# Selective scan on one core: the causal convolution as four shifted projections, D u as a diagonal product, and one output projection for each direction

## The chip, the core and the metric

The kernel runs on one core of a Trainium2 chip. The metric is the device time of one execution in microseconds, the median of several runs. All figures here come from the profile of one execution and from the times of the runs. TensorE is written PE, VectorE DVE, ScalarE ACT, GpSimd POOL and SyncE SP, as in the profile. L1392 is line 1392 of the kernel before.

## The reference

The program is a network of twelve blocks in a row: attention over a context with ternary weights, a bidirectional selective scan ("mamba"), grouped and expert feed-forward layers, three kinds of attention, a recurrent mixer. Only the scan block and the lines that prepare it change. The activations are 4 sequences of 128 tokens with 128 channels (512 tokens in all). The scan block adds to x the sum of two passes over the normalized x, one over the tokens in order and one over the tokens reversed (the reversed pass is turned back). One pass is, with 256 inner channels, 16 states and 4 taps:

```python
xi, z = jnp.split(x @ in_w.T, 2, axis=-1)
xc = conv_general_dilated(xc, conv_w, padding=[(3, 0)], feature_group_count=di)   # causal, 4 taps per channel
xc = silu(xc + conv_b)
x_dbl = xc @ xp_w.T                     # 8 columns dt, 16 of B, 16 of C
delta = softplus(dt @ dtp_w.T + dtp_b)
A = -jnp.exp(A_log)
h = h * exp(d_t * A) + (d_t * u_t) * b_t          # for each token, 256 x 16 states
y = einsum('bdn,bn->bd', h, c_t)
y = (y + xc * Dp) * silu(z)
return y @ out_w.T
```

## The kernel before

The program is written with Tile: the code gives instructions in program order, a scheduler lays them out in one fixed queue for each engine when the kernel is built, and semaphores are put in where a tile is handed over. The queue of an engine is not quite the order of the code (two dbu of neighbouring iterations stand next to one another at 210.23 us, ahead of the scans of the first), but on the chip each engine takes its queue as it stands. Tiles come from pools with a fixed number of buffers; a new tile of a pool waits until the one that it takes the place of has been read.

Everything in `mamba` is laid out with channels on partitions and the 512 tokens on the free axis. The 256 inner channels of a direction are two halves of 128. The stage runs from about 174 to 357 us of the span.

- **The pools.** All PSUM results except y and dA (xd_ps, xi_ps, z_ps, xdbl_ps, dt_ps, b_ps, c_ps, out_ps) come from one ring of three tiles, `ps`. y has its own tile of two halves, dA has three tiles. SBUF tiles of setup have two buffers, those of the loop (cs, dbu, h, hc) three.
- **setup(d)**, a generator, makes u, zs, x3, delta and du of a direction. Its first step transposes the normalized x with matmuls into xd_ps (L1304; with a flip for direction 1) and copies it to xT. For each half follows xi_ps (L1314, one matmul in fp32, two instructions in the profile), a copy by ScalarE into a tile with three zeros ahead of each sequence (pad, L1317), and the convolution on VectorE: one multiply by a scalar (L1321) and three multiply-adds (L1323). Silu on ScalarE gives u (L1325). Then z_ps and its silu (L1331, L1333), the projection xdbl_ps of u (L1337), copies of dt and x3 on VectorE (L1341 on; x3 is kept as three bf16 parts), dt_ps (L1355), the softplus (L1236 to L1255), and du = delta times u (L1363).
- **The loop.** For each direction and each of the 16 states n: b_ps and c_ps spread row n of B and of C over the partitions (L1368, PE), ACT copies c_ps to cs (L1381), DVE makes dbu = du times b_ps (L1383), ACT makes dA = exp(delta A) for each half (L1389), DVE scans each half (h, L1392), POOL multiplies h by cs (hc, L1395), and PE adds hc to y by a product with the identity (L1397, two fp32 matmuls). setup(1) is advanced by one step in each iteration from n = 2 of direction 0 on (`got = next(ahead, got)`), so all of its instructions stand among the loop's on every queue.
- **The end of a direction.** For each half, yd = u D + y on DVE (L1405) and yT = yd times zs (L1407).
- **The end of the stage.** After direction 1, 16 matmuls of 128x128 (two profile records each) project both directions into out_ps (L1413), and DVE adds it to x (L1416). The next stage (`grouped_ffn`) first reads x for its layer norm and loads ew from HBM on ACT's queue (L1430); SP's queue has the transfers r_qk and r_vo (L473), ctx (L1233), and w_r (L318).

`busy` (L389) issues matmuls with no use for the result, seven of them ahead of the first transpose. `load` fetches a weight tile once; the one of the scan block holds in_w, xp_w and out_w of both directions in one tile. In `bit_attention`, the stage before, several units of attention are processed in a loop over i, and after it a short chain (absmax, quantize to qf and qa, matmuls with ternary weights) ends the stage. `zero_after` makes a zero that depends on another value, so that what uses it waits.

Of the kernel before, what the change touches and what calls it, by code (L numbers as in the profile page):

```python
# [18 lines left out]
P = 128  # L19
B = 4  # L20
# [126 lines left out]
def _layout(i):  # L147
# [58 lines left out]
    def xp(m):  # L206
# [4 lines left out]
            i["L0_attn_in_w" + d].T, xp(i["L0_attn_xp_w" + d]), kchunks(i["L0_attn_out_w" + d].T))],  # L211
        axis=1,
    )
    a["dtp"] = np.concatenate([m.T for m in both("dtp_w")], axis=1)
    a["l0f"] = np.concatenate([i["L0_ffn_w1"], kchunks(i["L0_ffn_w2"])], axis=1)

# [55 lines left out]
class Net:  # L272
# [39 lines left out]
    def load(self, name):  # L312

        if name not in self._w:
            shape = list(self.A[name].shape)
            lo = XP - shape[0] if name == "dtp" else 0
            t = self.wp.tile([lo + shape[0]] + shape[1:], F32, tag="w", name="w_" + name)
            self.nc.sync.dma_start(t[lo:], self.A[name])  # L318
            self._w[name] = t
        return self._w[name]  # L320

    def copy(self, out, in_):
# [612 lines left out]
    def bit_attention(self, nxt):  # L935
# [4 lines left out]
        with ExitStack() as es:  # L940
# [211 lines left out]
            for i, u in enumerate(units):  # L1152
                u.top()
                if i + 1 < len(units):
                    units[i + 1].scores(0)
                u.spread()
                u.weights(0)
                u.weights(1)
                if i:
                    units[i - 1].values()  # L1160
                if i + 1 < len(units):
                    units[i + 1].scores(1)
                if i + 2 < len(units):
                    units[i + 2].queries()
                if i == 2:
                    ternary(ps, 5, 7)
                if i in (3, 4):

                    half = NS // 2
                    lo = (i - 3) * half  # L1170
                    mw = wk.tile([P, 1024], I32, tag="qtmp", name="mask")
                    nc.sync.dma_start(
                        mw[DC:AUG], self.A["mask"][:, lo // 4 : (lo + half) // 4].partition_broadcast(3)[:, 0])
                    aug = self.k("augs")[DC:AUG]
                    nc.gpsimd.tensor_scalar(
                        self.ctxT[DC:AUG, lo : lo + half], mw.bitcast(U8)[DC:AUG], aug[:, 0:1], aug[:, 1:2],
                        ALU.mult, ALU.add)
# [12 lines left out]
            self.quantize(wk, avg, qa, inv)  # L1190
            qab = one.tile([P, B, T], BF16, name="qab")
            nc.vector.tensor_copy(qab, bc_in(qa, T))
            hT = big.tile([P, BIG], F32, tag="big", name="hT")[:, 0 : 4 * N].rearrange("p (m n) -> p m n", m=4)
            osc = out_scale("f1", s)
            for m in range(4):
# [40 lines left out]
    def softplus(self, pool, out, vs, biases, first):  # L1236
# [4 lines left out]
        e = pool.tile([P, len(vs), N], F32, tag="sp_e", name="sp_e")  # L1241
        for i, (v, bias) in enumerate(zip(vs, biases)):
            nc.scalar.activation(e[:, i], v, AF.Abs, bias=bias)
            nc.vector.tensor_scalar(out[:, i], v, bias, 0.0, ALU.add, ALU.max)
        nc.scalar.activation(e, e, AF.Exp, scale=-1.0)
        s = pool.tile([P, len(vs), N], F32, tag="sp_s", name="sp_s")
        nc.vector.tensor_scalar_add(s, e, 1.0)
# [6 lines left out]
        nc.scalar.activation(s, s, AF.Ln)  # L1254
        nc.vector.tensor_add(out, out, s)  # L1255

    def mamba(self, nxt):

# [5 lines left out]
        with ExitStack() as es:  # L1266
# [17 lines left out]
            for j in range(3):  # L1284
                t = das.tile([P, B, T], F32, name=f"dA{j}")
                nc.vector.memset(t[:, :, 0:1], 0.0)
                dAs.append(t)
            turn = 0
            xn = one.tile([P, B, C], F32, name="xn")
            self.layernorm(self.x, xn)  # L1290
            yT = one.tile([P, 2, 2, N], F32, name="yT")
# [4 lines left out]
            def setup(d):  # L1296
# [6 lines left out]
                for b in range(B):  # L1303
                    nc.tensor.matmul(  # L1304
                        tr[:, b * T : b * T + T], xn[:, b], self.k("flip") if d else self.ident,
                        start=True, stop=True)
                xT = tp.tile([P, N], F32, tag="xT", name="xT")
                self.copy(xT, tr)
                yield
                u = wk.tile([P, 2, N], F32, tag="u", name="u")  # L1310
                for half in range(2):
                    i = d * 2 + half
                    mm = mm_tile("xi_ps")
                    nc.tensor.matmul(mm, w[:, at + half * P : at + half * P + P], xT, start=True, stop=True)  # L1314
                    pad = wk.tile([P, B, T + 3], F32, tag="pad", name="pad")
                    nc.gpsimd.memset(pad[:, :, 0:3], 0.0)
                    nc.scalar.copy(pad[:, :, 3:], mm.rearrange("p (b t) -> p b t", b=B))  # L1317
                    yield
                    cw = self.col("conv_w")[:, i * 4 : i * 4 + 4]
                    acc = wk.tile([P, B, T], F32, tag="conv", name="conv")  # L1320
                    nc.vector.tensor_scalar_mul(acc, pad[:, :, 0:T], cw[:, 0:1])  # L1321
                    for k in range(1, 4):
                        nc.vector.scalar_tensor_tensor(  # L1323
                            acc, pad[:, :, k : k + T], cw[:, k : k + 1], acc, ALU.mult, ALU.add)
                    nc.scalar.activation(  # L1325
                        u[:, half], self.flat(acc), AF.Silu, bias=self.col("conv_b")[:, i : i + 1])
                    yield
                zs = wk.tile([P, 2, N], F32, tag="z", name="z")
                for half in range(2):
                    mm = mm_tile("z_ps")  # L1330
                    nc.tensor.matmul(  # L1331
                        mm, w[:, at + 256 + half * P : at + 256 + half * P + P], xT, start=True, stop=True)
                    nc.scalar.activation(zs[:, half], mm, AF.Silu)  # L1333
                yield
                mm = mm_tile("xdbl_ps")
# [2 lines left out]
                        mm[:XP], w[:, at + 512 + half * XP : at + 512 + (half + 1) * XP], u[:, half],  # L1338
                        start=half == 0, stop=half == 1)
                dt = tp.tile([XP, N], F32, tag="dt", name="dt")  # L1340
                nc.vector.tensor_copy(dt[96:XP], mm[96:XP])  # L1341
                x3 = wk.tile([96, N], BF16, tag="x3", name="x3")
                r = tp.tile([96, N], F32, tag="x3r", name="x3r")
                nc.vector.tensor_copy(x3, mm[:96])
                nc.vector.tensor_sub(r[32:64], mm[32:64], x3[32:64])
                nc.vector.tensor_sub(r[64:96], mm[64:96], x3[64:96])
                nc.vector.tensor_copy(x3[32:64], r[32:64])
# [18 lines left out]
            def spread(x3, n, name):  # L1366
                mm = mm_tile(name)
                nc.tensor.matmul(mm, sel[:, n : n + 1].to_broadcast([96, P]), x3, start=True, stop=True)  # L1368
                return mm

            for got in setup(0):
                pass
            for d in range(2):
# [3 lines left out]
                for n in range(16):  # L1377
# [17 lines left out]
                    nc.gpsimd.tensor_mul(hc, h, bc_mid(cs, 2))  # L1395
                    for half in range(2):
                        nc.tensor.matmul(y[:, half], self.ident, hc[:, half], start=n == 0, stop=n == 15)  # L1397
                    if n > 1:
                        got = next(ahead, got)
                for got in ahead:  # L1400
                    pass
                for half in range(2):
                    i = d * 2 + half
                    yd = tp.tile([P, N], F32, tag="yd", name="yd")
                    nc.vector.scalar_tensor_tensor(  # L1405
                        yd, u[:, half], self.col("D")[:, i : i + 1], y[:, half], ALU.mult, ALU.add)
                    nc.vector.tensor_mul(yT[:, d, half], yd, zs[:, half])  # L1407
            out = mm_tile("out_ps").rearrange("p (b t) -> p b t", b=B)
            for b in range(B):
                for i in range(4):  # L1410
                    d, half = divmod(i, 2)
                    at = d * MW + 512 + 2 * XP + half * P
                    nc.tensor.matmul(  # L1413
                        out[:, b], yT[:, d, half, b * T : b * T + T], w[:, at : at + P],
                        start=i == 0, stop=i == 3)
            nc.vector.tensor_add(self.x, self.x, out)  # L1416

    def grouped_ffn(self, nxt):

# [831 lines left out]
```

## Time and profile before

| | us |
|---|---|
| median of the runs | 1392.51 (1391.57 to 1392.85, three runs) |
| the profiled execution's own time | 1393.84 |
| its span | 1391.7 |
| scan stage in the span | 174 to 357 |
| first dbu to the end of the last scan | 203.48 to 345.52 |
| last scan to the end of the residual add | 345.52 to 356.95 |

The granted TensorE clock is 0.916 of full speed over the whole span. In the stage the two directions' 64 scans and 32 dbu are the largest items of DVE, hc of POOL, and y of PE; dA is the largest of ACT.

How to read the lines that follow: in a group, "out<-in" are the program's tile names with shapes, then count, total busy time and mean time of one in nanoseconds, and after the second bar the time that its engine stood idle just before and the instruction that released it. In a timeline, the first number is the start, the second the duration, and the bracket at the end holds the idle time before. "x2" or more means neighbouring instructions joined.

### The profile page before, as it was taken

The numbers are of one execution on the slowest core, as the hardware profiler recorded it, in microseconds if no ns is written. First come the engines' busy times: TensorE is split into PE (matmuls) and PEld (weight loads), VectorE is DVE, ScalarE is ACT, GpSimd is POOL, SyncE is SP. The second block draws the span as 40 slices with busy tenths as digits, with TensorE's granted clock in tenths as the row PEclk, the third lists the DMA queues.
The fourth block names the chain that finished last, engine by engine and source line by source line (L and its number), as shares of the span: only waits on it lengthen the run. The fifth ranks groups of instructions, "written<-read, shape, count | busy, mean of one in ns | idle before, by whom it ended". The sixth has DMA issues, their size and how long they took to land.

```text
span 1391.7 us, 15803 instructions
## 1 busy us (share of the span) xinstructions
PE 1149.7 (83%) x6204; PEld 604.2 (43%) x6204; DVE 914.2 (66%) x1596; ACT 627.0 (45%) x848; POOL 205.9 (15%) x187
## 2 busy tenths in 40 slices
PE   2477557677899999999998944899987889999978
PEld 0156422222644444444433424476342454666644
DVE  7988779899348666776676698512564776554535
ACT  3743256444346555665553410233542761545432
POOL 0026205357000001000000430000122200000000
PEclk9988768789999999999999976799998988999978
DMA  6000000000700000000000100330000000000010
GB/s 188 0 1 2 1 1 0 30 0 0 211 0 1 0 0 0 1 0 0 1 1 0 61 0 1 104 75 23 0 0 7 7 7 0 2 1 2 3 57 8
DMA packets 9485, 27.82 MB, mean 20 GB/s; under 512 B 1191, under 2 KB 7120, under 8 KB 8350
## 3 DMA queue, kind: packets, MB, share of 16 engines
q1 hardware_dynamic: 8286, 24.88, 6.2%
q10 hardware_dynamic: 1120, 1.88, 0.4%
q8 instruction: 51, 0.84, 0.3%
q14 instruction: 28, 0.23, 0.1%
HBM read 26.49 MB, written 0.26 MB: 19 GB/s over the span
## 4 chain that ended last, share of the span: by engine, by line
PE 61%; DVE 19%; ACT 5%; issue 5%; POOL 3%; DVEq 0%; ACTq 0%; POOLq 0%
PE sc L590 12%; PE av L614 12%; PE s_ps L780 5%; DVE h L1392 3%; PE t_ps L804 2%; PE k_ps L706 2%; PE h_ps L1831 2%; PE y_ps L1843 2%; PE av L817 2%; PE mm L1478 2%; PE y_ps L1397 1%; DVE dbu L1383 1%; PE q_ps L542 1%; POOL hc L1395 1%; POOL mbs L606 1%
## 5 line engine op out<-in xcount | busy, mean ns | idle before, releaser
L614 PE MATMUL av<-s,ctx 128*97 128x512 f32 x448 | 210.4, 601 | 11.6 <-ACT s L612 11.0
L590 PE MATMUL sc<-q_aug,ctxT 99*128 99x512 f32 x448 | 206.2, 592 | 0.0
L611 DVE TENSOR_TENSOR s<-s,mbs 128x1024 f32<-128x1024 f32 x112 | 133.0, 1220 | 39.0 <-POOL mbs L606 39.0
L592 ACT COPY s<-sc 128x1024 f32<-128x1024 f32 x112 | 112.3, 1003 | 80.7 <-PE sc L590 80.7
L612 ACT ACTIVATE s<-s 128x1024 f32<-128x1024 f32 x112 | 116.2, 1057 | 63.1 <-DVE s L611 62.8
L600 DVE TENSOR_TENSOR m<-m,s 128x1024 f32<-128x1024 f32 x72 | 88.2, 1225 | 75.0 <-ACT s L592 75.0
L590 PEld LDWEIGHTS sc<-q_aug,ctxT 99*128 99x128 f32 x448 | 84.6, 189 | 110.2 <-issue 91.3
L614 PEld LDWEIGHTS av<-s,ctx 128*97 128x97 f32 x448 | 72.5, 166 | 124.1 <-issue 103.6
L784 DVE TENSOR_REDUCE na_m<-s_ps 128x1 f32<-128x512 f32 x128 | 82.2, 686 | 61.9 <-PE s_ps L780 61.7
L606 POOL PARTITION_ALL_REDUCE mbs<-m x20 | 35.7, 1785 | 488.4 <-DVE m L602 488.4
L810 ACT ACTIVATE p<-t_ps 128x1024 f32<-128x1024 f32 x64 | 62.0, 1021 | 85.4 <-PE t_ps L804 85.4
L1397 PE MATMUL y_ps<-hc,consts 128*128 128x512 f32 x128 | 75.6, 724 | 29.2 <-POOL hc L1395 27.7
L1395 POOL TENSOR_TENSOR hc<-h,cs 128x1024 f32<-128x1024 f32 x32 | 75.7, 2378 | 84.1 <-DVE h L1392 84.1
L780 PE MATMUL s_ps<-kT,q 32*128 32x512 f32 x256 | 81.9, 682 | 1.0 <-DVE na_m L784 0.9
L1392 DVE TENSOR_TENSOR_SCAN h<-dA,dbu 128x512 f32<-128x512 f32 x64 | 74.2, 1205 | 4.1 <-ACT dA L1389 3.9
L1397 PEld LDWEIGHTS y_ps<-hc,consts 128*128 128x128 f32 x128 | 26.1, 223 | 82.0 <-POOL hc L1395 56.4
L804 PE MATMUL t_ps<-q,kT 32*128 32x128 f32 x1024 | 57.0, 287 | 1.2 <-ACT p L810 1.2
L1389 ACT ACTIVATE dA<-delta,A 128x508 f32<-128x508 f32 x64 | 42.8, 687 | 29.5 <-DVE h L1392 29.3
L804 PEld LDWEIGHTS t_ps<-q,kT 32*128 32x128 f32 x1024 | 48.6, 189 | 11.2 <-issue 7.0
L393 PEld LDWEIGHTS <-consts 128*128 128x128 bf16 x160 | 17.6, 120 | 67.4 <-issue 51.3
L1847 DVE SCALAR_TENSOR_TENSOR x<-y_ps,cw,x 128x128 f32<-128x128 f32 x32 | 9.0, 345 | 50.3 <-PE y_ps L1843 44.4
L780 PEld LDWEIGHTS s_ps<-kT,q 32*128 32x128 f32 x256 | 28.1, 194 | 25.4 <-DVE na_m L784 14.8
(599 smaller groups left out, 1949.5 us busy)
## 6 DMA issues: line engine op xcount, KB each, us to landing
w_moe<-in_moe SPq DMA_DIRECT2D x2, 2048.0 KB, 9.6
ctxT<-in_ctxT SPq DMA_DIRECT2D x3, 768.0 KB
w_l3f<-in_l3f SPq DMA_DIRECT2D x1, 1920.0 KB, 8.1
rows<-in_rows ACTq DMA_DIRECT2D x1, 1664.0 KB, 13.7
w_l0f<-in_l0f SPq DMA_DIRECT2D x1, 1024.0 KB
w_mamba<-in_mamba SPq DMA_DIRECT2D x1, 976.0 KB, 18.3
w_r<-in_r SPq DMA_DIRECT2D x1, 960.0 KB
consts<-in_consts SPq DMA_DIRECT2D x1, 832.0 KB, 16.6
```

The lines of the kernel that those rows point to most:

```text
L590: nc.tensor.matmul(sc[:, i], self.ctxT[:, at : at + P], u.q, start=True, stop=True)
L592: nc.scalar.copy(s, sc)
L600: nc.vector.tensor_max(u.m, u.m, u.s[j])
L611: nc.vector.tensor_sub(p, p, bc_mid(u.mb, 2))
L612: nc.scalar.activation(p, p, AF.Exp)
L614: nc.tensor.matmul(u.av[: DC + 1], self.ctx[:, u.b * NCH + chunks[2 * j + i]], p[:, i], start=j + i == 0, stop=j == n - 1 and i == 1)
L780: nc.tensor.matmul(t, qs[rows], kT[rows, s, j * 512 : j * 512 + 512], start=True, stop=True)
L784: nc.vector.tensor_reduce(part[:, at : at + 1], t, axis=AX, op=ALU.max, negate=True)
L804: nc.tensor.matmul(ts[g // 2][:, g % 2, j], kT[g * 32 : g * 32 + 32, s, at : at + P], qs[g * 32 : g * 32 + 32], start=True, stop=True)
L1392: nc.vector.tensor_tensor_scan(h[:, half], self.flat(dA), dbu[:, half], 0.0, ALU.mult, ALU.add)
L1395: nc.gpsimd.tensor_mul(hc, h, bc_mid(cs, 2))
L1397: nc.tensor.matmul(y[:, half], self.ident, hc[:, half], start=n == 0, stop=n == 15)
```

## The change

- **Weights.** A 1 MB array `taps` with the convolution weights for each of four (direction, half) pairs and four taps, laid along the free axis, is added to the inputs. `load` fetches it to all partitions with a second transfer into the tile of the scan block. The load is called in `bit_attention` at i == 3. Weights of the projection times tap k give a stationary matrix for each tap (`conv_weights`): for half 0 of direction 0 VectorE computes it at the end of `bit_attention`, for the two halves of direction 1 POOL does so at the start of `mamba`.
- **The convolution.** For three of the four (direction, half) pairs, four matmuls with the tap matrices and the shifted padded xT accumulate the convolution in one PSUM tile, and silu reads it there. Half 1 of direction 0 keeps the convolution on VectorE. xT is written straight into the padded tile: for direction 0 one half by VectorE and one by ScalarE, for direction 1 by ScalarE.
- **ScalarE for direction 1.** The copies of dt and of x3 and the relu of the softplus go to ScalarE.
- **D u.** A diagonal matrix of D (`dd`, one multiply on POOL) times u is accumulated into y by two matmuls at n == 3 of each direction; yT is then y times zs.
- **The output projection.** Direction 0 is projected and added to x at n == 4 of direction 1, direction 1 at the end of the stage.

```diff
+    a["taps"] = np.concatenate([w.reshape(2, P, 4).transpose(0, 2, 1).reshape(-1) for w in both("conv_w")])[None]
@@ load
+            more = 16 * P if name == "mamba" else 0
+            t = self.wp.tile([lo + shape[0], shape[1] + more], F32, tag="w", name="w_" + name)
+            self.nc.sync.dma_start(t[lo:, : shape[1]], self.A[name])
...
+                taps = t[:, shape[1] :]
+                self.nc.sync.dma_start(taps, self.A["taps"].partition_broadcast(P)[:, 0])
@@ bit_attention
+                if i == 3:
+                    self.load("mamba")
...
             nc.vector.tensor_copy(qab, bc_in(qa, T))
+            self.conv_weights(0, self.taps[:, 0], s)
@@ softplus
-            nc.vector.tensor_scalar(out[:, i], v, bias, 0.0, ALU.add, ALU.max)
+            if first:
+                nc.vector.tensor_scalar(out[:, i], v, bias, 0.0, ALU.add, ALU.max)
+            else:
+                nc.scalar.activation(out[:, i], v, AF.Relu, bias=bias)
+    def conv_weights(self, i, out, x=None):
+        w, taps = self._w["mamba"], self.taps[:, i]
...
+        if x is None:
+            self.nc.gpsimd.tensor_mul(out, taps, w)
+        else:
+            self.nc.vector.scalar_tensor_tensor(out, taps, self.zero_after(x, "cv_z"), w, ALU.add, ALU.mult)
@@ mamba
+            cv = one.tile([P, 2, 4, P], F32, name="cvw")
+            for half in range(2):
+                self.conv_weights(2 + half, cv[:, half])
+            cvw = [self.taps[:, 0], None, cv[:, 0], cv[:, 1]]
+            for d in range(2):
+                pads.append(one.tile([P, B, T + 3], F32, name=f"pad{d}"))
+                nc.gpsimd.memset(pads[d][:, :, 0:3], 0.0)
+            dd = one.tile([P, 4, P], F32, name="dd")
+            nc.gpsimd.tensor_mul(dd, bc_mid(self.ident, 4), bc_in(self.col("D"), P))
...
-                xT = tp.tile([P, N], F32, tag="xT", name="xT")
-                self.copy(xT, tr)
+                xT = pad[:, :, 3:]
+                if d == 0:
+                    nc.vector.tensor_copy(xT[:, 0:2], tr[:, 0:2])
+                    nc.scalar.copy(xT[:, 2:4], tr[:, 2:4])
+                else:
+                    nc.scalar.copy(xT, tr)
                 yield
...
+                for half in (0, 1) if d else (1, 0):
...
+                    if i == 1:
...
+                    for k in range(4):
+                        nc.tensor.matmul(to, cvw[i][:, k], pad[:, :, k : k + T], start=k == 0, stop=k == 3)
+                    mms.append((half, mm))
+                    if d:
+                        silu(*mms.pop())
                     yield
...
-                nc.vector.tensor_copy(dt[96:XP], mm[96:XP])
+                (nc.scalar.copy if d else nc.vector.tensor_copy)(dt[96:XP], mm[96:XP])
-                nc.vector.tensor_copy(x3, mm[:96])
+                (nc.scalar.copy if d else nc.vector.tensor_copy)(x3, mm[:96])
...
+            def project(d):
+                out = mm_tile("out_ps").rearrange("p (b t) -> p b t", b=B)
+                for b in range(B):
+                    for half in range(2):
+                        at = d * MW + 512 + 2 * XP + half * P
+                        nc.tensor.matmul(
+                            out[:, b], yT[:, d, half, b * T : b * T + T], w[:, at : at + P],
+                            start=half == 0, stop=half == 1)
+                nc.vector.tensor_add(self.x, self.x, out)
...
                     for half in range(2):
                         nc.tensor.matmul(y[:, half], self.ident, hc[:, half], start=n == 0, stop=n == 15)
+                    if n == 3:
+                        for half in range(2):
+                            nc.tensor.matmul(y[:, half], dd[:, d * 2 + half], u[:, half], start=False, stop=False)
+                    if n == 4 and d:
+                        project(0)
                     if n > 1:
                         got = next(ahead, got)
...
-                    yd = tp.tile([P, N], F32, tag="yd", name="yd")
-                    nc.vector.scalar_tensor_tensor(
-                        yd, u[:, half], self.col("D")[:, i : i + 1], y[:, half], ALU.mult, ALU.add)
-                    nc.vector.tensor_mul(yT[:, d, half], yd, zs[:, half])
-            out = mm_tile("out_ps").rearrange("p (b t) -> p b t", b=B)
...
+                    nc.vector.tensor_mul(yT[:, d, half], y[:, half], zs[:, half])
+            project(1)
```

## Prediction

> **What bounds the kernel now.** I read the page's chain first: the span is mostly TensorE, and the stage that changes, from about 174 to 357 us, is one part of it. So I went to the costliest groups whose lines lie in that stage.
>
> ```profile
> PE 61%; DVE 19%; ACT 5%; issue 5%; POOL 3%; DVEq 0%; ACTq 0%; POOLq 0%
> ...
> L1397 PE MATMUL y_ps<-hc,consts 128*128 128x512 f32 x128 | 75.6, 724 | 29.2 <-POOL hc L1395 27.7
> L1395 POOL TENSOR_TENSOR hc<-h,cs 128x1024 f32<-128x1024 f32 x32 | 75.7, 2378 | 84.1 <-DVE h L1392 84.1
> L1392 DVE TENSOR_TENSOR_SCAN h<-dA,dbu 128x512 f32<-128x512 f32 x64 | 74.2, 1205 | 4.1 <-ACT dA L1389 3.9
> L1389 ACT ACTIVATE dA<-delta,A 128x508 f32<-128x508 f32 x64 | 42.8, 687 | 29.5 <-DVE h L1392 29.3
> ```
>
> The scans on VectorE waited 4.1 us in all; TensorE, GpSimd and ScalarE waited for them far longer. VectorE sets the pace of the scan loop. The table of stretches says how tight that is:
>
> ```profile
> 203.50:244.00 40.50, 28.93 (x61) 11.79 (x61) 38.43 (x35) 24.19 (x36) 19.53 (x8) 0.79 0.00 1
> 244.00:282.00 38.00, 24.67 (x43) 8.13 (x41) 30.85 (x31) 17.29 (x25) 12.65 (x6) 0.76 0.08 28
> 282.00:350.00 68.00, 49.10 (x112) 17.78 (x112) 63.29 (x58) 30.07 (x50) 43.54 (x19) 0.95 0.00 0
> ```
>
> The first number after the stretch is its length, then PE, PE loads, DVE, ACT, POOL busy, and the clock granted to TensorE. VectorE is busy 38.4 of 40.5 us in the first stretch, but TensorE already has 28.9 there at a mean clock of 0.79: room for about 11 us more, if its order allows it.
>
> In the undisturbed loop (first of each pair of dbu at 308.34, 315.06, 321.78) two iterations take 6.72 us, all VectorE: 32 iterations are 107.5 of the 142.0 us from the first dbu (203.48) to the end of the last scan (345.52). The other 34.5 are about 25 us of the second direction's setup and the first one's gating on VectorE, and 9.3 of its idle time.
>
> **What comes off VectorE.** In the groups of VectorE inside the loop:
>
> ```profile
> L1323 DVE SCALAR_TENSOR_TENSOR conv<-pad,cols,conv 128x512 f32<-128x512 f32 x6 | 6.3, 1050 | 0.0
> L1321 DVE TENSOR_SCALAR conv<-pad,cols 128x512 f32<-128x512 f32 x2 | 2.9, 1450 | 0.0
> L1244 DVE TENSOR_SCALAR delta<-dt_ps,cols 128x512 f32<-128x512 f32 x2 | 1.4, 734 | 0.0
> ```
>
> By the steps between starts, the eight convolution instructions cost 8.6 us (some wait for GpSimd before they work). dt and x3 move to ScalarE (0.73 + 0.61), so do the two relus (1.3): 11.2 us of VectorE saved in direction 0's loop. In direction 1 two yd (L1405) and their handoff go: 2.2. Were VectorE still the only limit, this and the tail would be the gain.
>
> **What TensorE gets, and in which order.** Direction 1's convolution becomes eight fp32 matmuls in place of two, the D u product two per direction. In TensorE's queue of the changed program, what stands ahead of the fourth iteration's b_ps (on which dbu, and so both scans wait) is: two shifted matmuls, y of n=2 and of n=3, two D u, two shifted matmuls, b_ps. Before, one xi_ps stood there, and the y's came after:
>
> ```profile
> 217.12 0.38 PE L1368 MATMUL b_ps<-x,sel 96*128 96x512 bf16 x1
> ...
> 217.54 1.22 DVE L1383 TENSOR_TENSOR dbu<-du,b_ps 128x1024 f32<-128x1024 f32 x1 [0.51 <-PE b_ps L1368]
> 217.56 1.88 PE L1397 MATMUL y_ps<-hc,consts 128*128 128x512 f32 x4
> ...
> 219.60 1.98 PE L1397 MATMUL y_ps<-hc,consts 128*128 128x512 f32 x4 [0.16 <-POOL hc L1395]
> ```
>
> A warm fp32 matmul of 512 columns is two records 0.43 apart, 0.86 us. I replayed the queues by hand with these durations:
> - n=4: y of n=3 starts at 219.60 as before; then six matmuls (y 2, D u 2, shifted 2) of 0.86 and a b_ps of 0.43: dbu at 225.4 instead of 217.54. VectorE has no other ready work, so it stands still about 8.4 us.
> - n=5: three shifted matmuls, then y of n=4, one shifted, b_ps. Its y needs the whole chain: dbu 1.2, two scans 2.3, hc 2.36, y 1.72, shifted 0.86, b_ps 0.43, so dbu of n=5 comes 9 us after that of n=4 where 3.36 is the work: a stall of 5.6. The ring of three PSUM tiles gives no slack: the xi tile holds a place.
> - n=7: y of n=5 and the first xdbl ahead of it: 3.2.
>
> That is 17 us of new waits. Against it stand the 11.2, and some of the old 9.3 us of stalls (before, 1.83 for xdbl_ps, and 2.67 and 1.56 around the table loads), which either shrink or lie beside the new ones. ScalarE gets two more table loads (1.28 each, silu and exp three times in place of two) and 2.7 us of copies and relus, less two pad copies of 0.59; it is busy 24 of 40 us, so only those on the dA path count, which my replay has. The replay puts dbu of n=14 at 279.9 to 281.0, with warm clock, and 280.9 is where it was.
>
> **A rule on the clock.** The replay's chain hc, y, b_ps leaves TensorE idle 2.3 us at a time. The trace, in the table of stretches and the timeline:
>
> ```profile
> 238.40:241.80 3.40, 1.45 (x4) 0.26 (x2) 2.44 (x3) 3.14 (x5) 1.99 (x1) 1.00 0.00 0
> 241.80:245.20 3.40, 2.98 (x4) 1.43 (x5) 2.34 (x2) 2.42 (x4) 0.75 (x2) 0.50 0.00 0
> ...
> 242.22 3.46 PE L1397 MATMUL y_ps<-hc,consts 128*128 128x512 f32 x4 [1.23 <-POOL hc L1395]
> ```
>
> A window with 1.45 us of matmuls, no gap in it longer than 1.23, was followed by one at half clock, where the y pair cost 3.46 in place of 1.98. The Trainium skill ("TensorE: Matmul & The Clock Gate", Part 1) says that the clock drops after about 3.4 us idle. By that rule none of the new waits is long enough, and direction 0 comes out even (+0). By the row, one of the chain's windows goes cold, +1 to +2. I follow the row: +1.0; rule instead of row would take 1 us off the sum.
>
> **Direction 1.** Saved: 2.2. New: the residual add in the loop, 0.75. project(0) puts eight output matmuls (0.244 each, 2 us) ahead of y of n=2 and n=3, the two D u, y of n=4 and then b_ps of n=5; the residual add stands ahead of h of n=4 on VectorE, and hc, y of n=4 follow it. The stall before dbu of n=5 is 4.7, and up to 1 for the clock (take 0.25). Net +3.5.
>
> **The tail.**
>
> ```profile
> 345.60 2.34 POOL L1395 TENSOR_TENSOR hc<-h,cs 128x1024 f32<-128x1024 f32 x1 [1.14 <-DVE h L1392]
> 348.00 1.98 PE L1397 MATMUL y_ps<-hc,consts 128*128 128x512 f32 x4 [1.50 <-POOL hc L1395]
> 350.02 0.75 DVE L1405 SCALAR_TENSOR_TENSOR yd<-u,cols,y_ps 128x512 f32<-128x512 f32 x1 [4.50 <-PE y_ps L1397]
> ...
> 353.05 3.17 PE L1413 MATMUL out_ps<-w_mamba,yT 128*128 128x128 f32 x26 [1.02 <-DVE yT L1407]
> ...
> 356.26 0.69 DVE L1416 TENSOR_TENSOR x<-x,out_ps 128x512 f32<-128x512 f32 x1
> ```
>
> Two yd (0.75 each) leave this chain, yT reads PSUM directly, and of the 13 output matmuls after the last yT seven remain: 1.5 + 1.45 = -2.95. The next stage's transfers start from the same points on SP's and ACT's queues: r_qk still waits for the last yT, so 1.5 earlier; ew no longer does. ews waited for ew until 356.02, which would cap the gain if ew did not move; it does move.
>
> **First setup, the stage before.** Direction 0's two convolution halves run on different engines now (one on VectorE, one on TensorE), so xdbl_ps comes 1.8 us earlier with a warm clock (its four records took 3.65 at half clock). The split copy of xT costs +0.14, the wait and instruction for cv_z in bit_attention +0.1 (the STT of 0.72 hides in the 0.84 us that qab waits; uncovered it would be 0.7). GpSimd now multiplies 128x512 three times (1.26 each by L1118) just where layernorm runs on VectorE; where the two met in the loop, an STT of 0.72 took 1.71. Taken +1.3, ends 0.5 and 2.6. Net -0.3. The taps transfer (1 MB more) stands on SP's queue right behind w_mamba, which went out at 7.02. The transfers were at full rate (about 317 GB/s) until 24 us, so it lands near 28, over 130 us before its first use, and VectorE reads ctxT from 11.4 us on without a wait for a transfer: zero; at worst 1 MB at that rate, 3.3 us, on what lands before it.
>
> **A rule on GpSimd.** In the trace GpSimd goes from partition reductions (168.86) to the multiplies of the scan loop (208.17, 0.08 after its scan), and no row shows a cost of the switch; but 39 us lay between. The skill ("GPSIMD Engine Reference", Instruction dispatch) says that the first call of a freshly loaded kernel pays about 6 us that no row shows. That speaks against the change: its multiplies now come at 175, and pad's memset, which the first shifted matmuls need at 181.7, stands behind them. Without a charge the memset is done at 177.9; charged from the last reduction on, at 180.7; charged at the first call, 183.8, a loss of 2.1. Zero to +2.1; I take zero, the row's.
>
> **Sum.** -0.3 + 1.0 + 3.5 - 2.95 = +1.3 us, on the profiled execution's 1393.84 that is 1395.1; its own time stands 1.3 over the median of 1392.51, so against the median 1393.8, said as 1394. A difference of 0.2% (2.8 us) is about what a measurement of this kernel can tell from none.
>
> **Rivals.**
> 1. VectorE stays the bound: the waits at n=4, 5, 7 are filled because matmuls flow better than I replay (the hc chain is already late, or several y's bunch). Then 11.2 + 2.2 + 2.95 + 0.3 less the residual add's 0.75, 15.9 us, come off; with 40% of the new waits (17 + 4.7) left, 8.7, that is -7.2: about 1385; with none left, 1376.6. For: 38.4 of 40.5 us. Against: the order of TensorE's queue. Chance 0.20.
> 2. Slower: the clock. The point is whether a 3.4 us window with an hc wait holds less than about 1.5 us of matmuls. If it happens at three links (y of n=4 and of n=5, and direction 1's y of n=4), each costs about 2 more than in the sum: +6, about 1400; with late weights or GpSimd's load on top 1402. For: seven such spells in this stage already, clock 0.76 to 0.79. Against: ten more fp32 matmuls keep it busier. Chance 0.22.
>
> The forecast has 0.58, with 1390 to 1398 as its own range; a third of it lies above 1395.3. So faster 0.22, same 0.33, slower 0.45. The range that holds 8 in 10 is 1386 to 1402.
>
> **What would show it.** Right: a dbu near n=4 waiting 6 to 9 us for b_ps and the next 4 to 6, one of 4 to 5 in direction 1 after its residual add; scans' end to x add near 8.4 in place of 11.4; PEclk at 0.8 in the first stretch. Wrong: VectorE idle in the loop still below 12 us, which is rival 1; y pairs of over 3 us in more than two of those chains, rival 2; a shifted matmul waiting for a GpSimd memset past 182, the load; or a wait on the taps transfer.

## The result, and the profile after

The changed kernel takes 1400.75 us in the median of 15 runs (1392.3 to 1407.9); the kernel before, run beside it, 1392.6 (1390.9 to 1394.8). The ratio is 1.0054, interval 1.0036 to 1.0071: slower by 5.0 to 9.9 us. The profiled execution took 1401.26 us, its span 1399.3 at a granted clock of 0.907. One execution at a clearly lower clock than the others of its kernel (370.8 us at 0.814, of the changed kernel ended after the stage) is left out of the figures below.

The costliest groups of the stage, in the page of the changed kernel (the lines of the file have moved: L1463 is the scan, L1454 dbu, L1466 hc, L1468 y):

```profile
L1468 PE MATMUL y_ps<-hc,consts 128*128 128x512 f32 x128 | 72.4, 698 | 33.0 <-POOL hc L1466 33.0
L1466 POOL TENSOR_TENSOR hc<-h,cs 128x1024 f32<-128x1024 f32 x32 | 75.4, 2366 | 94.6 <-DVE h L1463 90.1
L1463 DVE TENSOR_TENSOR_SCAN h<-dA,dbu 128x512 f32<-128x512 f32 x64 | 74.0, 1204 | 2.8 <-ACT dA L1460 2.1
...
L1454 DVE TENSOR_TENSOR dbu<-du,b_ps 128x1024 f32<-128x1024 f32 x32 | 37.6, 1206 | 23.6 <-PE b_ps L1429 23.4
```

The scans and hc cost what they did. What is new is the last line: VectorE stood idle for 23.6 us ahead of dbu, for b_ps from TensorE; before, this wait was 0.5. The stretches of the stage (length, then PE, PE loads, DVE, ACT, POOL busy, clock) show where:

```profile
204.48:245.00 40.52, 29.46 (x65) 12.15 (x65) 24.11 (x21) 19.33 (x26) 14.02 (x6) 0.84 0.00 0
245.00:282.00 37.00, 25.43 (x47) 8.28 (x46) 30.06 (x29) 22.04 (x33) 14.54 (x6) 0.76 0.08 29
282.00:354.00 72.00, 53.04 (x135) 20.30 (x133) 65.77 (x60) 33.59 (x55) 45.20 (x20) 0.95 0.00 0
```

In the first stretch of the loop VectorE is busy 24.1 of 40.5 us, where it was busy 38.4. The timeline at n=4 of direction 0 (start, duration) is the queue that the prediction laid out:

```profile
217.08 1.88 PE L1381 MATMUL xi_ps<-pad,cvw 128*128 128x512 f32 x4
...
218.80 3.78 PE L1468 MATMUL y_ps<-hc,consts 128*128 128x512 f32 x8
...
222.41 1.88 PE L1471 MATMUL y_ps<-u,dd 128*128 128x512 f32 x4
224.13 1.88 PE L1381 MATMUL xi_ps<-pad,cvw 128*128 128x512 f32 x4
225.85 0.38 PE L1429 MATMUL b_ps<-x,sel 96*128 96x512 bf16 x1
...
226.27 1.22 DVE L1454 TENSOR_TENSOR dbu<-du,b_ps 128x1024 f32<-128x1024 f32 x1 [8.24 <-PE b_ps L1429]
...
235.59 1.22 DVE L1454 TENSOR_TENSOR dbu<-du,b_ps 128x1024 f32<-128x1024 f32 x1 [5.64 <-PE b_ps L1429]
```

Ten fp32 products (20 records) stand ahead of one b_ps, whose result 8.2 us of idle VectorE waited for; at n=5 it is 5.6. The end of the stage is shorter:

```profile
353.25 2.34 POOL L1466 TENSOR_TENSOR hc<-h,cs 128x1024 f32<-128x1024 f32 x1 [1.16 <-DVE h L1463]
355.65 1.98 PE L1468 MATMUL y_ps<-hc,consts 128*128 128x512 f32 x4 [1.51 <-POOL hc L1466]
357.67 1.29 DVE L1479 TENSOR_TENSOR yT<-y_ps,z 128x512 f32<-128x512 f32 x2 [4.50 <-PE y_ps L1468]
...
358.42 2.42 PE L1437 MATMUL out_ps<-w_mamba,yT 128*128 128x128 f32 x16 [0.79 <-DVE yT L1479]
...
360.88 0.69 DVE L1440 TENSOR_TENSOR x<-x,out_ps 128x512 f32<-128x512 f32 x1 [0.91 <-PE out_ps L1437]
```

From the end of the last scan to the end of the residual add it is 8.4 us in place of 11.4. Read off the two timelines, the spans compare so:

| stretch | before | changed | difference |
|---|---|---|---|
| start to the end of `bit_attention` | 175.03 | 178.17 | +3.1 |
| to the first dbu (first setup) | 28.45 | 26.32 | -2.1 |
| to the first dbu of direction 1 | 84.15 | 87.24 | +3.1 |
| to the end of the last scan | 57.89 | 61.45 | +3.6 |
| to the end of the residual add | 11.42 | 8.39 | -3.0 |
| the ten blocks behind it | 1034.8 | 1037.7 | +3.0 |

The stage itself is 1.5 us longer. Some 6 of the 7.6 us of this pair of profiles lie outside of it, nearly all in code that the change does not touch (cv_z and the tap weights in `bit_attention` are the exception; the last x there ends 6.2 us after the start of the last am_h_g in both). The first row of the table is not to be taken for a cost of the change: in the profiles of the runs below, `bit_attention` ends between 174.1 and 179.0 us where the code up to there is that of the kernel before, and between 174.7 and 178.2 us where it is that of the change.

### The profile page after: what moved, and what is told of

It reads as the page before. It is cut to its first block, busy times and chain, and to the rows that moved or that the text cites. A ratio compares the mean times of both kernels' runs of the same rounds, so it can differ in the third digit from the quotient of the medians.

```text
span 1399.3 us, 15834 instructions
## 1 busy us (share of the span) xinstructions
PE 1157.2 (83%) x6219; PEld 608.1 (43%) x6230; DVE 899.0 (64%) x1579; ACT 630.5 (45%) x852; POOL 208.3 (15%) x189
## 4 chain that ended last, share of the span: by engine, by line
PE 62%; DVE 17%; issue 5%; ACT 5%; POOL 4%; DVEq 0%; ACTq 0%; POOLq 0%
PE sc L598 12%; PE av L622 12%; PE s_ps L788 5%; DVE h L1463 3%; PE t_ps L812 3%; PE k_ps L714 2%; PE h_ps L1895 2%; PE y_ps L1468 2%; PE y_ps L1907 2%; PE av L825 2%; PE mm L1542 2%; POOL hc L1466 2%; PE q_ps L550 1%; POOL mbs L614 1%; DVE dbu L1454 1%
## 5 line engine op out<-in xcount | busy, mean ns | idle before, releaser
L1468 PE MATMUL y_ps<-hc,consts 128*128 128x512 f32 x128 | 72.4, 698 | 33.0 <-POOL hc L1466 33.0
L1466 POOL TENSOR_TENSOR hc<-h,cs 128x1024 f32<-128x1024 f32 x32 | 75.4, 2366 | 94.6 <-DVE h L1463 90.1
L1463 DVE TENSOR_TENSOR_SCAN h<-dA,dbu 128x512 f32<-128x512 f32 x64 | 74.0, 1204 | 2.8 <-ACT dA L1460 2.1
L1468 PEld LDWEIGHTS y_ps<-hc,consts 128*128 128x128 f32 x128 | 25.0, 213 | 79.9 <-POOL hc L1466 60.4
L1454 DVE TENSOR_TENSOR dbu<-du,b_ps 128x1024 f32<-128x1024 f32 x32 | 37.6, 1206 | 23.6 <-PE b_ps L1429 23.4
```

The source lines that it names most:

```text
L1463: nc.vector.tensor_tensor_scan(h[:, half], self.flat(dA), dbu[:, half], 0.0, ALU.mult, ALU.add)
```

## The experiments

The changed kernel differs from the kernel before in the stage, in the 1 MB transfer at the start, and in cv_z. The first two runs ask whether the transfer makes what lies outside of the stage.

**The transfer alone, on the kernel before.**

```diff
+            more = 16 * P if name == "mamba" else 0
+            t = self.wp.tile([lo + shape[0], shape[1] + more], F32, tag="w", name="w_" + name)
...
+            if more:
+                self.nc.sync.dma_start(t[:, shape[1] :], self.A["taps"].partition_broadcast(P)[:, 0])
```

> The kernel before, with the 1 MB taps transfer added behind w_mamba and read by nothing. In the trace of the changed kernel the scan stage costs 1.5 us more, while 3.1 us more lie ahead of it and 3.0 behind it, in code that is the same. If the transfer makes these (it holds up the ctxT transfers at the start by about 1 us, and shifts what follows against the windows of the TensorE clock): 3 to 7 us slower than before, with times spread over 8 us or more. If the stage itself is at the bottom of it: within 1 us of before, with times as close together as before's (4 us).

Measured: ratio 0.9997 (0.9985 to 1.0008), 1393.6 us beside 1394.2. The transfer costs nothing that can be measured (at most 1.1 us).

**The transfer held back, on the changed kernel.**

```diff
-                taps = t[:, shape[1] :]
+                taps = t[:, shape[1] :]; self.nc.vector.tensor_copy(taps[:, 0:1], late)
...
-                    self.load("mamba")
+                    self.load("mamba", fused[:, 0:1])
```

> The changed kernel with its taps transfer held back until a first column of fused is written (about 100 us), so that the start has the transfers of before. If the start makes the difference outside of the stage: 1.0 to 2.5 us slower than before (the stage's own 1.5), spread 4 us. If not: 7 us slower as the changed kernel, spread over 8 us or more.

Measured: ratio 1.0077 (1.0055 to 1.0099), 1398 to 1408 us, although the transfer now went out at 115 us in place of 11. Both runs say the same: the transfer at the start is not the cause.

**Direction 1's convolution back on VectorE.**

```diff
-                    if i == 1:
+                    if i >= 1:
...
-                        cw = self.col("conv_w")[:, 4:8]
+                        cw = self.col("conv_w")[:, i * 4 : i * 4 + 4]
...
+                        if d:
+                            silu(*mms.pop())
+                            yield
```

> The changed kernel with both halves of direction 1's convolution back on VectorE, all else as changed. Theory of TensorE's queue: the dbu of n=4 no longer waits 8.2 us for b_ps (under 1), n=5 waits about 4 less the convolution that fills it, so from the first dbu of direction 0 to the first of direction 1 is 84 to 86 us, against 87.2 changed and 84.2 before, although 8.6 us of VectorE work are back. Theory that VectorE is the bound: 8.6 us longer than changed, 95 us. Direction 1 as changed, 57.8 us to its last dbu.

Measured: ratio 0.9977 (0.9960 to 0.9993), so 3.2 us faster than before, and from the first dbu of direction 0 to that of direction 1 82.3 us (84 to 86 expected), with 8.6 us of VectorE work back in it. VectorE's timeline of this run:

```profile
218.00 1.22 DVE L1457 TENSOR_TENSOR dbu<-du,b_ps 128x1024 f32<-128x1024 f32 x1 [1.46 <-PE b_ps L1432]
...
223.11 3.47 DVE L1376 SCALAR_TENSOR_TENSOR conv<-xi,cols,conv 128x512 f32<-128x512 f32 x2
230.88 1.22 DVE L1457 TENSOR_TENSOR dbu<-du,b_ps 128x1024 f32<-128x1024 f32 x1 [4.30 <-PE b_ps L1432]
```

The wait at n=4 fell from 8.24 to 1.46 us (under 1 expected), the one at n=5 is 4.30, and the convolution's instructions stand between them. The theory that VectorE is the bound expected 95 us. Direction 1 is unchanged (58.0 us). By the two ratios this kernel is 11 us faster than the changed one; its profile has 4.5 of them in the stage (178.9 us in place of 183.4) and 5.7 behind it.

**Without the diagonal product.** D u is added on VectorE again.

```diff
-                    if n == 3:
-                        for half in range(2):
-                            nc.tensor.matmul(y[:, half], dd[:, d * 2 + half], u[:, half], start=False, stop=False)
...
-                    nc.vector.tensor_mul(yT[:, d, half], y[:, half], zs[:, half])
+                    nc.vector.scalar_tensor_tensor(
+                        yd, u[:, half], self.col("D")[:, d * 2 + half : d * 2 + half + 1], y[:, half], ALU.mult, ALU.add)
+                    nc.vector.tensor_mul(yT[:, d, half], yd, zs[:, half])
```

> The changed kernel without the diagonal product: D u is added on VectorE as before, all else as changed. Queue theory: two matmuls less ahead of b_ps of n=4, its dbu waits 6.5 in place of 8.2; in direction 1 the 4.7 us wait falls to under 2; yd comes back, 2.2 at the change of direction and 1.5 in the tail. Stage 1 to 2 us shorter than changed. Theory that VectorE is the bound: the stage is 3.7 longer.

Measured: ratio 1.0023 (1.0010 to 1.0035), 1397.3 us. The wait at n=4 is the 6.5 us that the queue theory gave, and the one in direction 1 is gone (the line below). But the stage is 183.7 us, 0.3 longer than changed, where 1 to 2 less was expected: the wait at n=5 rose from 5.6 to 7.1 us, and the returning yd's took 2.9 us in the tail, where 1.5 was expected. That the kernel as a whole is 4 us faster than the changed one lies behind the stage (1031.8 us in its profile, 1037.7 in that of the changed kernel). VectorE's waits in direction 1 (waiting instruction, releaser, us in total, times, longest):

```profile
DVE dbu L1452 <- PE b_ps L1427: 0.9, 1, 0.9
```

**One output projection at the end.**

```diff
-                    if n == 4 and d:
-                        project(0)
...
-                            start=half == 0, stop=half == 1)
+                            start=i == 0, stop=i == 3)
```

> The changed kernel with one output projection at the end as before, all else as changed. Queue theory: in direction 1 the 2 us of output matmuls and the residual add leave the queue ahead of b_ps of n=5, so its wait falls from 4.7 to about 2 and direction 1 from 57.8 to 54.5 us; the tail gets its eight matmuls back (1.5 to 2 us). If the two D u products alone make the wait: direction 1 stays at 57 or more.

Measured: ratio 1.0046 (1.0024 to 1.0068), 1398.9 us. The interval holds the 1.0054 of the changed kernel. The wait stands:

```profile
DVE dbu L1455 <- PE b_ps L1429: 4.8, 1, 4.8
```

From its first to its last dbu, direction 1 takes 55.1 us in place of 57.8. That is no gain of this size: here, as in the run before this one and in the two at the end, the last two dbu stand next to one another in VectorE's queue, ahead of the scans of the first. To the end of the last scan, direction 1 takes 60.8 us in place of 61.5. With the run before it splits direction 1's loss: the y's with the two D u products between them make this wait (0.9 without D u), and the residual add of the early projection costs 0.7 us beside it. The expectation that the wait would fall to 2 was wrong.

**The two kernels, ended after the stage.** The blocks behind it and their transfer of rows are left out, so that the time up to there is known in several executions.

```diff
-        for i, (block, args) in enumerate(BLOCKS):
+        for i, (block, args) in enumerate(BLOCKS[:2]):
...
-            if i == 1:
-                net.load_rows(es)
```

> The kernel before, ended after the scan stage: the ten blocks behind it are left out and x is written out. Its queue of TensorE up to that point is the same. It gives the time up to the end of the stage in many executions, not only in the profiled one: about 362 us (357 to the residual add, and the transfer of the output), spread of 3 us.

> The changed kernel, ended after the scan stage in the same way. If the stage costs in every execution what the profiles show (1.5 us more) and the rest of the loss lies in the blocks behind it: 1.0 to 3 us above the cut kernel before, with the same spread. If the stage itself is longer in other executions than in the profiled one (the clock in the chain of waits): 5 to 9 us above it, spread 6 or more.

Measured: before 362.0 to 366.9 us, mean 364.2 (five executions); changed 364.8 to 367.7, mean 366.2 (five). So the end of the stage comes 2.0 us later; by the two ratios to the kernel before, which ran beside both, it is 2.2, give or take 1.4, which agrees with the 1.5 of the profiles and with the first expectation. The whole kernels differ by 7.5: about 5 us, give or take 3, must lie behind the stage. The profile of the cut changed kernel, the longest of the five, shows where the stage can cost more. Its direction 0 took 83.4 us to the dbu of n=14 (80.5 in the full one; 77.4 before, 78.4 in the cut kernel before), and the matmul that dbu of n=5 depends on was slow:

```profile
231.31 2.93 PE L1468 MATMUL y_ps<-hc,consts 128*128 128x512 f32 x4 [2.11 <-POOL hc L1466]
234.03 1.82 PE L1381 MATMUL xi_ps<-pad,cvw 128*128 128x512 f32 x2
```

The same two take 1.98 and 1.02 us in the full kernel (at 232.50 and 234.32), 1.75 less. This is the half clock on the chain, the second rival, in one execution and not in another.

**Delays.** Three, two, and on the changed kernel four multiplications of 128x512, ahead of the last output projection. (The clock of TensorE is halved for 3.4 us at a time or for a multiple of it in these traces, but for one spell at the end of each; the expectations call such a stretch a window.)

```diff
+            for _ in range(3):
+                nc.vector.tensor_scalar_mul(yT[:, 1, 1], yT[:, 1, 1], 1.0)
```

> The kernel before with three multiplications by one of 128x512 put on the chain between the last yT and the output projection, 1.4 us of pure delay, nothing else. If the blocks behind the stage take a time that depends on when they start (the windows of the TensorE clock): not 1.4 us slower but 4 to 8, or faster. If they do not: 1.0 to 2.0 us slower.

> The kernel before with two of the three added multiplications, 0.9 us of delay ahead of the output projection. In the profiles of the kernel before the residual add ends 2.1 to 2.5 us after the start of a window of the TensorE clock (3.41 us long), in those of the changed kernel 3.1 to 4.0 after it. If the place in the window at which the next blocks begin makes the rest of the loss: 4 to 7 us slower than before. If not: 0.9, at most 2.5 with a cold output projection as in the run with three.

> The changed kernel with four such multiplications, 1.8 us of delay, ahead of its last output projection; that brings the end of the stage to where the kernel before has it in the window. If the place in the window matters: no slower than the changed kernel (7.5 above before), 2 to 6 above before. If not: 1.8 to 3.5 slower than the changed kernel, 9 to 11 above before.

Measured: with three 1.0004 (0.9989 to 1.0019), with two 1.0025 (1.0015 to 1.0035), on the changed kernel with four 1.0068 (1.0048 to 1.0087). In the profiles the end of the stage moved by 3.0, 2.6 and 2.9 us, more than the added work: the matmuls of the projection then ran in part at half clock (granted 0.50 from 353.3 to 356.7 us with three multiplications, after 2.4 us in which TensorE stood idle; before, after 1.0 us, it was 1.00). The output matmuls with three multiplications, 4.75 us where they took 3.17:

```profile
353.34 4.75 PE L1415 MATMUL out_ps<-w_mamba,yT 128*128 128x128 f32 x26 [2.40 <-DVE yT L1409]
```

On the kernel before, neither run came out clearly as one of its two expectations. The delay of 3.0 us cost 0.5 us (-1.5 to 2.6), the one of 2.6 us cost 3.5 (2.1 to 4.9). They differ by 2.9 us, give or take 2.5, so the time of the blocks behind seems to depend on when they start. On the changed kernel, the delay that should have brought it to 2 to 6 us above the kernel before left it 9.5 above (6.7 to 12.1). So the place in the window at which the scan stage ends does not explain the changed kernel.

**Rearranged.** What shortens a chain is kept, what lengthens TensorE's queue ahead of b_ps is not: the convolution of direction 1 is on VectorE as in the third run, and D u and the early projection stand later. First:

```diff
-            for half in range(2):
-                self.conv_weights(2 + half, cv[:, half])
...
+                    if n == 15 and d:
+                        project(0)
...
-                    if n == 3:
+                    if n == 14 and not d:
...
+                for half in range(2 if d else 0):
+                    nc.tensor.matmul(y[:, half], dd[:, 2 + half], u[:, half], start=True, stop=False)
```

> The parts of the change that shorten a chain, without those that lengthen TensorE's queue ahead of b_ps: direction 1's convolution on VectorE (its tap weights are not made), D u at n=14 of direction 0 and as the first product into y of direction 1, direction 0's output projection at n=15 of direction 1, all else as changed. Queue theory: direction 0 as with the convolution on VectorE (75.5 us to the dbu of n=14), direction 1 no wait of 4.7, the two yd's handoff saved and one residual add more: 53 to 55 us in place of 57.8 and 54.2; tail 8.4. Stage 5 to 7 us shorter than before, time 1386 to 1390. If VectorE is not the bound even without those waits: no better than with the convolution on VectorE alone (1388.5).

Measured: ratio 0.9974 (0.9958 to 0.9989), 1390.1 us, no faster than with the convolution on VectorE alone (0.9977), which was the mark of the second expectation. But a wait had come back. The profiled stage is 175.3 us in place of 181.9 (that execution took 1384.4 us, 5.7 under the median), and direction 1 had a new wait of 4.9 us at n=4, since the scheduler put the two D u products and the eight y products of n=0 to n=3 ahead of one b_ps. So D u of direction 1 was moved to n=14 too:

```diff
-                    if n == 14 and not d:
+                    if n == 14:
...
-                for half in range(2 if d else 0):
-                    nc.tensor.matmul(y[:, half], dd[:, 2 + half], u[:, half], start=True, stop=False)
```

> As the rearranged kernel, with D u of direction 1 also at n=14 in place of the start, so that no bundle of y products stands ahead of a b_ps at the change of direction (the rearranged kernel still waited 4.9 us there). Queue theory: no wait for b_ps of over 2 us in direction 1, 52 to 54.5 us from its first to its last dbu (54.2 before, 57.8 changed), tail 8.4; the stage 8 to 11 us shorter than before, time 1382 to 1387. If something other than the queue holds direction 1: stage as with the rearranged kernel, 175.3, time 1389 to 1391.

Measured: ratio 0.9905 (0.9883 to 0.9927), 1381.9 us beside 1394.0, faster than both kernels. The stage is 172.2 us, 9.7 shorter than before. To the end of its last scan, direction 1 takes 55.0 us (57.9 before, 61.5 changed); from its first dbu to its last it is 49.4, less than expected because the last two dbu stand together. In the group of dbu the wait is mostly gone (4.3 of what is left are at n=7 of direction 0):

```profile
L1454 DVE TENSOR_TENSOR dbu<-du,b_ps 128x1024 f32<-128x1024 f32 x32 | 37.6, 1206 | 4.7 <-PE b_ps L1429 4.6
```

D u stands at the end, where no b_ps waits behind it. But the last y does:

```profile
335.96 4.66 POOL L1468 TENSOR_TENSOR hc<-h,cs 128x1024 f32<-128x1024 f32 x2 [2.05 <-DVE h L1463]
...
338.37 1.98 PE L1470 MATMUL y_ps<-hc,consts 128*128 128x512 f32 x4 [0.86 <-POOL hc L1468]
340.19 1.88 PE L1473 MATMUL y_ps<-u,dd 128*128 128x512 f32 x4
341.91 0.61 PE L1437 MATMUL out_ps<-w_mamba,yT 128*128 128x128 f32 x4
342.35 1.88 PE L1470 MATMUL y_ps<-hc,consts 128*128 128x512 f32 x4
```

The last hc is done at 340.62 and its y starts at 342.35, 1.7 us later (1.3 behind the D u products, 0.4 behind two products of the output projection); in the changed kernel it is 0.05. So from the end of the last scan to the end of the residual add it is 10.1 us, where 8.4 was expected: a better place for D u of direction 1 is still to be found.

## Why the prediction was right or wrong

**The mechanism was right.** The work taken from VectorE was given back as waits for b_ps behind TensorE's queue. By place, predicted and measured: n=4 8.4 and 8.24; n=5 5.6 and 5.64; direction 1 4.7 and 4.72. Direction 1 as a whole +3.5 and +3.6, the tail -2.95 and -3.0. Most of the stage's sum, +1.3 and +1.5, is luck: two of its terms were off by about 2 us, one up and one down. The third run showed the mechanism: with 8.6 us of work put back on VectorE the wait at n=4 all but went, and the stage became 4.5 us shorter than changed. The last run used it.

**Direction 0 was too low by 2 us.** Predicted +1.0, measured +3.1 in the profile, +3.3 and +3.3 in two others of the same stage, and 6.0 in the cut one. The step is n=7, 3.2 predicted and 4.84 measured: both halves of xdbl stood ahead of its b_ps, not one, and the y of n=5 ran for 3.21 us, in part at half clock:

```profile
241.83 3.21 PE L1468 MATMUL y_ps<-hc,consts 128*128 128x512 f32 x4 [2.76 <-POOL hc L1466]
...
245.27 2.18 PE L1398 MATMUL xdbl_ps<-u,w_mamba 128*104 128x512 f32 x4
...
247.70 1.22 DVE L1454 TENSOR_TENSOR dbu<-du,b_ps 128x1024 f32<-128x1024 f32 x1 [4.84 <-PE b_ps L1429]
```

I had counted one cold window (a spell at half clock) for 1 us over the whole direction. Of the prediction's row and rule on the clock, the row held: TensorE was idle for 2.76 us ahead of this y, less than 3.4. The older waits of VectorE in direction 0, 9.0 us before, still came to 4.7, where the replay had left about 3.

**The first setup was too high by 1.8.** Predicted -0.3, measured -2.1. For 1.3 of it the term is that of GpSimd's multiplications beside the layer norm; the rest is open. They did not meet: GpSimd started after it, probably for a reason that the second rule of the prediction had named and that I had set to zero:

```profile
172.00 0.35 POOL L911 PARTITION_ALL_REDUCE am_h_g<-am_h_m  x1 [7.90 <-DVE am_h_m L908]
175.06 0.11 POOL L1370 MEMSET xi<- 128x12 f32 x1 [2.71 <-DVE qh L941]
182.11 2.48 POOL L1278 TENSOR_TENSOR cvw<-w_mamba 128x512 f32<-128x512 f32 x2 [6.94 <-PE xd_ps L1343]
184.54 0.15 POOL L1324 MEMSET pad<- 128x12 f32 x2
```

The multiplications wait for nothing later than the last x of the stage before, which was done at 178.17 (the xd_ps that the profile names as releaser is no input of theirs). So 3.9 us passed that no instruction or wait accounts for. In the nine runs that have this switch there, 6.8 to 7.3 us lie between the memset and the first multiplication, with a wait in them or without. The price was small, since the shifted matmuls then waited only 0.34 us for pad's memset, and the delay kept GpSimd clear of the layer norm. So the rule on GpSimd (the Trainium skill, "GPSIMD Engine Reference", Instruction dispatch: about 6 us for the first call of a freshly loaded kernel) agrees with the trace where I took zero, though no run shows that the time is spent on loading. The trace before could not show it, with 39 us between the two kinds of work.

**The sum left out what is not in the stage, and that is most of why 1394 was wrong by 6.8 us.** The changed kernel lies inside the range of 1386 to 1402, and slower was the likeliest sign, but most of the amount came from a place that none of the three cases named; that the range held it is in part luck. The cut kernels put the end of the stage at +2; some 5 us are behind it, in ten blocks that have the same instructions. I gave this no term. What the runs show of it: among the changed kernel's 15 runs time and clock went together (0.921 at 1392.3 us, 0.899 at 1407.9). In the profiles, the blocks behind the stage took 1037.2 to 1041.2 us, and in them the stage of narrow attention 162.0 us in all three that carry the whole change and a projection for each direction (changed, transfer held back, with delay). In the other nine of full kernels they took 1029.2 to 1034.8 and 157.9 to 159.2. The stage of narrow attention before and changed, with the columns of the stretches above:

```profile
1156.33:1314.21 157.88, 155.26 (x2097) 98.54 (x2096) 89.94 (x160) 68.28 (x88) 0.00 (x0) 0.96 0.01 2
```

```profile
1163.87:1325.90 162.03, 159.34 (x2097) 101.19 (x2096) 89.89 (x160) 68.31 (x88) 0.00 (x0) 0.93 0.01 2
```

The count of matmuls is the same, the clock 0.93 in place of 0.96. In all twelve profiles of full kernels the clock is halved there once, near the stage's start: for 23.9 us in those three, for 13.7 or 17.1 us in the nine. Before and changed:

```profile
1160.01:1173.66 13.65, 12.57 (x54) 7.43 (x55) 8.90 (x16) 0.00 (x0) 0.00 (x0) 0.50 0.00 0
```

```profile
1167.51:1191.40 23.89, 22.46 (x139) 13.55 (x136) 13.89 (x23) 3.88 (x4) 0.00 (x0) 0.50 0.00 1
```

The length goes with the place at which narrow attention starts. The halved clock sets in 4.71 to 4.76 us after the first s_ps matmul in the three, 3.05 to 3.11 us after it in those with 17.1, and 5.87 to 6.38 us after it in those with 13.7, except that the kernel before, with 13.7 too, stands at 4.82, next to the three. These are twelve single executions, and no run moved that start alone, so this is not shown to be the cause. What puts the start there in these three kernels is open; the transfer and the place of the scan stage's end in a clock window were tried and are not it.

**The rivals.** The first (VectorE stays the bound) did not happen for the change; the last run shows that its 1385 was within reach when the waits were taken away. The second happened in part: half clock on the chain at n=5 in one execution (1.8 us by the two groups shown), and at n=7 in the profile (1.2 us on the y), not six.

## What to carry to other kernels

Work that moves from a bound engine to one with idle time is worth what the order of that engine's queue makes of it: count the instructions that stand between a late result and the next instruction for which the bound engine waits, and give the moved work a place behind the last such instruction, not the first free one. Ten fp32 products ahead of one b_ps cost 8.2 us; at the end of direction 1 two D u and two output products cost 1.7, since there the last y waits behind them. And two kernels can differ in code that is the same: end both after the changed stage before the rest is explained by it.

## What was not expected of the hardware

- The switch of GpSimd from reductions and memsets to multiplications took about 7 us (6.8 to 7.3 in nine runs), with no instruction in them. In the last run, where the multiplication for dd follows the memsets, the profile puts this idle time down to nothing:

```profile
183.51 1.03 POOL L1324 TENSOR_TENSOR dd<-consts,cols 128x512 f32<-128x512 f32 x1 [7.28 <-issue]
```

- 1.35 us of multiplications ahead of the output projection moved its end by 3.0, for the matmuls that followed ran in part at half clock, and the whole kernel was then not measurably slower.
- A stage with the same matmuls was at half clock for 13.7, 17.1 or 23.9 us in different runs, in step with where it started against the changes of the clock.
- The changed kernel's times spread over 16 us from one execution to the next, along with the granted clock (before, 4 us in the same runs, and 10 us over 36 others).
